# Paired exponentials over a ring of score chunks in a multi-expert attention stage

## The chip, the cores and the metric

The kernel runs on one core of a Trainium2 chip. The core has five engines that run side by side, each with its own instruction queue in program order: TensorE (PE, with its weight loads shown apart as PEld), VectorE (DVE), ScalarE (ACT), GpSimd (POOL) and SyncE (SP, which here issues DMAs). Semaphores tie them together: an instruction that needs another engine's result waits at the head of its queue, and everything behind it waits as well.

The metric is device time in microseconds (us) of one launch. Before the change it is 2863.09 us, the median of three runs (2863.0 to 2865.14).

## The reference, cut to what matters

A two-layer network on 3327 tokens with 256 features. Each layer is a graph step followed by a feed-forward block. The last block, `_L1_ffn_ref`, is the one that matters here. It is an attention with 4 heads of 64 features, and for each head 4 "experts", which have queries of their own but share keys and values:

```python
q = jnp.einsum('bnsd,neod->bneso', sx, wq)
k = jnp.einsum('bnsd,nod->bnso', sx, wk)
v = jnp.einsum('bnsd,nod->bnso', sx, wv)
causal = jnp.where(jnp.tril(jnp.ones((s, s), bool)), 0.0, -jnp.inf).astype(x.dtype)
scores = jnp.einsum('bnesd,bntd->bnest', q, k) * d ** 0.5 + causal
att = jax.nn.softmax(scores, axis=-1)
qkv = jnp.einsum('bnest,bntd->bnesd', att, v)
```

After it the experts are mixed by a gate, and a normalization, two small matrix products, a second normalization and a last gate follow. All of it is float32.

## The kernel before

The work is cut into 26 token tiles of 128 rows. The first stages (graph step, mixture of experts, second graph step) fill about the first 985 us. The change lies in the last stage, the method `heads`.

**Units and chunks.** A unit is one token tile `t` and one head `h`: 104 units in order of `t`, then `h`. Because attention is causal, a unit's keys are tiles 0 to `t`. They are cut into `t // 4 + 1` chunks of at most four tiles (512 columns), made about even by `span`. There are 392 chunks in one list, and a chunk is written `(u, g)`, with `g` its number in the unit.

**What happens to a chunk.** Five helpers work on it:

- `fill`: TensorE makes the scores of four experts in four PSUM banks (`pqk`), which all small products of the stage share.
- `drain`: VectorE copies the four score blocks out of PSUM into a tile `sc` of 4 x 512 columns and takes each row's maximum (`mx`). Where the chunk is the unit's last, it adds the causal mask, and the negated maximum over all chunks, `nmax` (in the profile `anmax`), is made.
- `weigh`: ScalarE takes the exponential in place, one instruction for each expert, and adds each row up into `den` (in the profile `aden`). Each such instruction is followed by a read of the accumulator. It needs `nmax`, and so the drains of all chunks of the unit.
- `turn`: VectorE transposes the chunk in 32 x 32 blocks, all four experts in one instruction.
- `attend`: TensorE multiplies the turned weights with the values `vr`, fetched by SP from DRAM, and adds up in one PSUM area `po`.

When a unit ends, `over` copies `po` to `ot` (ScalarE) and masks it (GpSimd), or does both on VectorE for `t` under 5; `back`, a round later, multiplies it with a matrix and ScalarE copies the result, `qkv`.

**Rounds.** The order of the work is written out by hand in one loop over the chunks, and a wrapper (`InOrder`) keeps each engine's instructions in the order in which the code makes them. One round, for chunk `k`, does: drain ahead; `attend` chunk `k`; `turn` the next chunk, or from tile 5 to about tile 23 the one after it (`extra`); fetch values; the first two exponentials of a chunk ahead (chunk `k + 2 + extra(k)`), if it is not the first of its unit; `back` and `over` where they are due; one step of the preparation of the next token tile (`run(preps)`) and one step of each unfinished tail (`run(tails)`); the remaining exponentials of the chunk ahead; ScalarE's small put-off operations (`quiet`); one `fill`. In a round that follows a unit's end, from tile 8 on, `run(preps)` and `run(tails)` are left out. A chunk with `g == 0` gets all four exponentials at the later place.

A tail is a generator that takes a finished token tile through gate, normalizations and small products, a step a round. Steps that matter for GpSimd's queue are the third (the gate's weights, products with `qkv` and sums into `fx`), the seventh and a later one (a normalization: `l1ns`, `l1rs`, `fx`, later `l2ns`, `l2rs`, `fo`), and `nonzero`, a comparison (`nz`, `nzf`).

**Buffers.** `sc` tiles come from a pool of nine buffers (`scp`); a buffer is used again when `attend` has read it. The queries of the first five token tiles (`qts`) are also kept in tiles of this pool. `den` has three buffers and is not cleared: each of its columns is written by one exponential.

Of the kernel before, what the change touches and what calls it, by code (L numbers as in the profile page):

```python
# [12 lines left out]
F32 = mybir.dt.float32  # L13
# [9 lines left out]
P = 128  # L23
# [5 lines left out]
BLK = 512  # L29
# [72 lines left out]
class Net:  # L102
# [753 lines left out]
    def heads(self, xs, vs, out):  # L856
        tc, a = self.tc, self.a
        nc = InOrder(tc)
        Q = 32
        with ExitStack() as ctx:  # L860
            one = ctx.enter_context(tc.tile_pool(name="at", bufs=1))
            self.work = ctx.enter_context(tc.tile_pool(name="atw", bufs=2))
            scp = ctx.enter_context(tc.tile_pool(name="ats", bufs=9))
            vrp = ctx.enter_context(tc.tile_pool(name="atv", bufs=3))
            tl = ctx.enter_context(tc.tile_pool(name="att", bufs=2))
            sm = ctx.enter_context(tc.tile_pool(name="atsm", bufs=4))
# [5 lines left out]
            )  # L872

            kt = one.tile([P, 4, NP], F32, name="kt")


            load = dict(act=0.0, dve=0.0)
# [30 lines left out]
            def prepare(t, res):  # L908
# [77 lines left out]
                yield  # L986
                if t < AHEAD:

                    qt = scp.tile([P, 4, BLK], F32, tag="sc", name="qts")[:, :, : 2 * P]
                    qt = qt.rearrange("p h (i q) -> p h i q", i=2)  # L990
                else:
                    qt = tl.tile([P, 4, 2, P], F32, tag="qt", name="qt")
# [42 lines left out]
            def span(t, g):  # L1035


                n = t // 4 + 1
                lo, hi = (t + 1) * g // n, (t + 1) * (g + 1) // n
                return lo, hi - lo  # L1040
# [15 lines left out]

            def drain(u, g):

                n = span(u["t"], g)[1] * P
                last = g == u["t"] // 4  # L1060
                if g == 0:
                    u["sc"] = {}
                    u["mx"] = sm.tile([P, 4, 8], F32, tag="mx", name="mx")
                sc = u["sc"][g] = scp.tile([P, 4, BLK], F32, tag="sc", name="sc")
                for e in range(4):
                    s, m = u["pq"][e][:, :n], u["mx"][:, e, g : g + 1]
                    if last:
                        nc.vector.tensor_tensor_reduce(
                            sc[:, e, :n], s, mask[:, BLK - n :], 1.0, NEG, ALU.add, ALU.max, m
                        )  # L1070
                    else:
                        nc.vector.tensor_scalar(
                            sc[:, e, :n], s, 1.0, None, ALU.mult, ALU.max, accum_out=m
                        )
                    load["dve"] += 0.12 + 0.00104 * n
                if last:
                    u["nmax"] = sm.tile([P, 4], F32, tag="nmax", name="anmax")
                    nc.vector.tensor_reduce(
                        u["nmax"], u["mx"][:, :, : g + 1], AX.X, ALU.max, negate=True
                    )  # L1080
                    load["dve"] += 0.2

            def weigh(u, g, experts):

                n = span(u["t"], g)[1] * P
                q = ready[u["t"]]
                if u["h"] == g == 0 and 0 in experts:
                    q["den"] = sm.tile([P, 16, 7], F32, tag="den", name="aden", bufs=3)
                for k in experts:
                    e = u["sc"][g][:, k, :n]  # L1090
                    nc.scalar.activation(
                        e, e, AF.Exp, bias=u["nmax"][:, k : k + 1],
                        accum_out=q["den"][:, 4 * u["h"] + k, g : g + 1],
                    )
                    load["act"] += 0.26 + 0.00088 * n

            def values(u, g):

                lo, n = (4 * i for i in span(u["t"], g))
                v = u["v", g] = vrp.tile([P, 16, 64], F32, tag="vr", name="vr")  # L1100
                for q in range(4):
                    nc.sync.dma_start(out=v[ds(Q * q, Q), :n, :], in_=vs[u["h"], :, lo : lo + n, :])

            def turn(u, g):


                n = span(u["t"], g)[1] * P
                w = u["sc"][g][:, :, :n]
                nc.vector.transpose(w, w)
                load["dve"] += 0.1 + 0.00417 * n  # L1110

# [6 lines left out]
            def attend(u, g):  # L1118


                t = u["t"]
                w, v = u["sc"][g], u["v", g]
                lo, n = (4 * i for i in span(t, g))
                for b2 in range(0, n, 2):
                    for k in range(2):
                        for q in range(4):
                            r, b = ds(Q * q, Q), b2 + k

                            after = 4 * t + q - lo
                            if b > after and t:  # L1130
                                continue
                            nc.tensor.matmul(
                                po[ds(64 * k, 64), q, :, :], v[r, b, :], w[r, :, ts(b, Q)],
                                start=(g == b2 == 0), stop=(b + 2 > after if t else b2 == 2),
                            )
# [307 lines left out]
                nc.sync.dma_start(out=out[ts(t, P), :], in_=fo)  # L1443

            units = [dict(t=t, h=h) for t in range(NT) for h in range(4)]
            chunks = [(u, g) for u in units for g in range(u["t"] // 4 + 1)]
            def begin(u):

                t = u["t"]
                if u["h"] == 0:  # L1450
                    if t == 0:
                        for _ in prepare(0, ready.setdefault(0, {})):
                            quiet()
                    while preps and "qt" not in ready[t]:
                        run(preps)
                        quiet()
                    begun = [t + 1] if AHEAD <= t + 1 < NT else []
                    if t + 2 < AHEAD:
                        begun = [t + 2] if t else [1, 2]
                    for i, n in enumerate(begun):  # L1460
                        preps.append(later(4 * i, prepare(n, ready.setdefault(n, {}))))
                u.update(ready[t])
# [3 lines left out]
            def fill_next():  # L1466
                nonlocal filled
                if filled < len(chunks):
                    u, g = chunks[filled]
                    if g == 0:  # L1470
                        begin(u)
                    fill(u, g)
                    filled += 1

            def drain_to(n):
                nonlocal drained
                while drained < min(n, len(chunks)):
                    if filled == drained:
                        fill_next()
                    drain(*chunks[drained])  # L1480
                    drained += 1

            def extra(k):

                t = chunks[min(k + 3, len(chunks) - 1)][0]["t"]
                return int(chunks[k][0]["t"] >= 5 and t // 4 + 1 <= 6)

            def wanted(k):

                c = min(k + 2 + extra(k), len(chunks) - 1)  # L1490
                return k + 3 + extra(k) + chunks[c][0]["t"] // 4
# [4 lines left out]
            drain_to(wanted(0))  # L1496
            for k in range(2):
                values(*chunks[k])
                weigh(*chunks[k], range(4))
            turn(*chunks[0])  # L1500
            fill_next()
            ended, flipped, weighed = None, 1, 2
            for k, (u, g) in enumerate(chunks):
                drain_to(wanted(k))
                attend(u, g)
                while flipped < min(k + 2 + extra(k), weighed, len(chunks)):
                    turn(*chunks[flipped])
                    flipped += 1
                if k + 2 < len(chunks):
                    values(*chunks[k + 2])  # L1510
                rest = []
                while weighed < min(k + 3 + extra(k), len(chunks)):
                    c = chunks[weighed]
                    if c[1]:
                        weigh(*c, range(2))
                    rest.append((*c, range(2 if c[1] else 0, 4)))
                    weighed += 1
                if ended:
                    back(ended)
                last = u if g == u["t"] // 4 else None  # L1520
                if last:
                    over(u)
                if not ended or u["t"] < 8:
                    run(preps)
                    run(tails)
                ended = last
                for c in rest:
                    weigh(*c)
                quiet()
                if filled == drained:  # L1530
                    fill_next()
# [557 lines left out]
```

## Time and profile before

The profiled execution took 2863.94 us by itself, with a span of 2862.2 us, and lies 0.85 us above the median of the three runs.

| engine | busy us | share of the span | in the 1650 us from 1150 to 2800 |
|---|---|---|---|
| TensorE | 2665.0 | 93% | 1607.63 |
| VectorE | 2368.9 | 83% | 1600.73 |
| ScalarE | 1790.0 | 63% | 1237.74 |
| GpSimd | 1075.3 | 38% | 599.39 |

How to read the profile. "Busy" counts an instruction from its start to its end. TensorE's matmuls are pipelined and their ends are modelled, so its busy share says little about how near it is to its limit. A group of instructions is shown as line, engine, operation, what is written and from what, shapes and count; then the busy time in us, the mean of one in ns, and the idle time of the engine just before, with what ended it. All instructions of this stage have the wrapper's line, L61, so they are told apart by the names of their tiles. A line of waits tells who waited for whom: us in total, how many times, the longest. A line of the timeline tells the start in us, the duration, the engine, the instruction, and in brackets the idle time before it with what ended it. The chain that ended last is followed back from the last instruction to what released it, step by step.

### The profile page before, as it was taken

What the parts mean: (1) busy time and instruction counts of PE and PEld (TensorE: products, weight loads), DVE (VectorE), ACT (ScalarE), POOL (GpSimd) and SP (SyncE); (2) the same over time, 40 slices, a digit from 0 to 9 for tenths busy, and PEclk for the clock granted to TensorE, in tenths of its full rate; (3) what the DMA queues carried; (4) which work ended last, traced back from release to release, by engine and by line L of the source; (5) the groups of instructions that cost most, each with busy time, mean ns of one, the idle gap of its engine ahead of it and who ended that gap; (6) DMA issues with size and microseconds to landing.
All of it is one profiled execution on the core that took longest, in us unless ns stands there. A gap on an engine that the chain in (4) does not pass through costs nothing.

```text
span 2862.2 us, 125012 instructions
## 1 busy us (share of the span) xinstructions
PE 2665.0 (93%) x53422; PEld 1979.1 (69%) x53422; DVE 2368.9 (83%) x5525; ACT 1790.0 (63%) x5130; POOL 1075.3 (38%) x1562
## 2 busy tenths in 40 slices
PE   7999988878989899999999999999999999999995
PEld 5888877756767666676666666666666666666664
DVE  5203643589999588899999999999999999999996
ACT  6510135555555367777777777777777777777774
POOL 5541644532132137755444333333233222223122
PEclk9999999999999799999999999999999999999998
DMA  9994568657775232333433443434343444434332
GB/s 381 388 337 138 180 217 266 209 183 247 275 273 180 73 94 84 109 108 116 116 111 113 119 121 114 116 118 121 114 127 116 120 120 119 123 116 122 117 107 78
DMA packets 258188, 449.69 MB, mean 157 GB/s; under 512 B 58816, under 2 KB 156608, under 8 KB 257504
## 3 DMA queue, kind: packets, MB, share of 16 engines
q1 hardware_dynamic: 245536, 417.50, 46.0%
q0 software_dynamic: 6576, 18.02, 1.7%
q8 instruction: 420, 6.88, 1.0%
q10 hardware_dynamic: 5520, 6.18, 0.6%
q14 instruction: 136, 1.11, 0.1%
HBM read 393.37 MB, written 25.88 MB: 146 GB/s over the span
## 4 chain that ended last, share of the span: by engine, by line
DVE 35%; PE 28%; ACT 3%; issue 2%; POOL 1%; DMA 0%; SPq 0%; POOLq 0%; DVEq 0%; ACTq 0%
DVE sc L61 32%; PE pqk L61 10%; PE po L61 10%; PE acc L61 2%; ACT sc L61 2%; PE ptO L61 2%; PE psxt L61 1%; PE pt L61 1%; PE pq L61 1%; PE ph L61 0%; ACT sq L61 0%; PE pk L61 0%; PE pv L61 0%; DVE anmax L61 0%; DVE gl L61 0%
## 5 line engine op out<-in xcount | busy, mean ns | idle before, releaser
L61 ACT ACTIVATE sc<-sc,anmax 128x512 f32<-128x512 f32 (+3 forms) x1568 | 1041.4, 669 | 102.9 <-DVE anmax L61 102.9
L61 PEld LDWEIGHTS po<-sc,vr 32*64 32x64 f32 x43728 | 662.5, 131 | 299.1 <-issue 147.6
L61 DVE STREAM_TRANSPOSE sc<-sc 128x2048 f32<-128x2048 f32 (+3 forms) x392 | 816.0, 2082 | 9.7 <-ACT sc L61 9.4
L61 PE MATMUL po<-sc,vr 32*64 32x128 f32 x43728 | 761.1, 276 | 31.6 <-DVE sc L61 21.5
L61 PE MATMUL pqk<-kt,qt 64*128 64x512 f32 (+1 forms) x2944 | 764.4, 585 | 19.0 <-DVE fgs L61 6.6
L61 DVE TENSOR_SCALAR_CACHE_REDUCE sc<-pqk 128x512 f32<-128x512 f32 (+2 forms) x1152 | 653.1, 621 | 26.0 <-PE pqk L61 23.8
L61 PEld LDWEIGHTS pqk<-kt,qt 64*128 64x128 f32 x2944 | 315.9, 185 | 239.5 <-issue 80.9
L61 PE MATMUL acc<-wh,p 128*128 128x259 f32 x1352 | 309.2, 386 | 35.6 <-DVE p L61 35.6
L61 PEld LDWEIGHTS acc<-wh,p 128*128 128x128 f32 x1352 | 253.2, 190 | 93.4 <-DVE p L61 53.3
L61 PE MATMUL acc<-y,pan 128*128 128x256 f32 x1352 | 298.4, 382 | 1.7 <-issue 1.7
L61 ACT ACTIVATION_READ_ACCUMULATOR sc<-sc,anmax 128x1 f32 x1568 | 299.5, 191 | 0.0
L61 PEld LDWEIGHTS acc<-y,pan 128*128 128x128 f32 x1352 | 257.2, 191 | 38.7 <-issue 3.2
L61 POOL TENSOR_TENSOR ot<-ot,sxd 128x512 f32<-128x512 f32 x83 | 105.9, 1276 | 436.2 <-ACT ot L61 431.1
L61 DVE CUSTOM_DVE_ANT_0 sc<-pqk,mask 128x512 f32<-128x512 f32 (+3 forms) x416 | 241.9, 636 | 25.4 <-PE pqk L61 24.6
L61 ACT ACTIVATE u<-u,d 128x512 f32<-128x512 f32 (+1 forms) x182 | 125.2, 688 | 159.2 <-DVE u L61 159.1
L61 DVE SCALAR_TENSOR_TENSOR u<-bc,d 128x512 f32<-128x512 f32 (+1 forms) x182 | 136.0, 748 | 0.1
L61 DVE SCALAR_TENSOR_TENSOR p<-pan,u 128x512 f32<-128x512 f32 (+1 forms) x182 | 126.1, 693 | 10.3 <-PE acc L61 6.1
L61 ACT COPY qkv<-ptO 128x272 f32<-128x272 f32 x104 | 39.7, 381 | 131.0 <-PE ptO L61 130.8
L61 PE MATMUL ptO<-igw,ot 128*128 128x68 f32 x832 | 115.7, 282 | 3.8 <-DVE sc L61 2.1
L61 PEld LDWEIGHTS ptO<-igw,ot 128*128 128x128 f32 x832 | 101.5, 192 | 22.5 <-issue 15.2
L61 ACT ACTIVATE junk<-ar 128x1664 bf16<-128x1664 f32 x52 | 82.8, 1592 | 54.1 <-DMA ar<-in_adj_dram 53.6
L61 DVE CUSTOM_DVE_ANT_0 sg<-sg,dst 128x1664 bf16<-128x1664 bf16 (+2 forms) x56 | 100.1, 1796 | 1.2 <-ACT dst L61 1.0
(356 smaller groups left out, 3082.0 us busy)
## 6 DMA issues: line engine op xcount, KB each, us to landing
vr<-vs SPq DMA_DIRECT2D x976, 128.0 KB
ar<-in_adj_dram SPq DMA_DIRECT2D x104, 832.0 KB
vr<-vs SPq DMA_DIRECT2D x544, 96.0 KB
pan<-in_adjt_dram SPq DMA_DIRECT2D x156, 256.0 KB
pan<-in_adjt_dram SPq DMA_DIRECT2D x26, 1024.0 KB
pan<-in_adjt_dram SPq DMA_DIRECT2D x20, 832.0 KB
w1e<-w SPq DMA_DIRECT2D x59, 256.0 KB
took<-places SPq DMA_DIRECT2D x59, 129.0 KB
```

Of the source, the lines that this page charges most:

```text
L61: made = make(*args, **kw)
```

## The change

The nine score buffers become one tile, `ring`, with the four experts as rows of 9 x 512 columns. Chunk number `c` has slot `c % 9`, and `c % 6` for the first 24 chunks, while the queries of the first five token tiles lie in the last three slots. Two neighbouring chunks of a unit, an even `g` and the one after it, form a pair where their slots are neighbours. The first of a pair is put at the right end of its slot, so that an expert's scores of both chunks lie side by side, and one exponential takes both, with one sum for both. The columns of `den` that no exponential writes any more have to be zero, so `den` is cleared by GpSimd for each token tile. Where a pair does not begin a unit, its first two exponentials are put into the round ahead, one early and one late, and the other two into its own round, again one early and one late. Chunks without a partner are treated as before. `turn` and `attend` go on chunk by chunk.

```diff
-            scp = ctx.enter_context(tc.tile_pool(name="ats", bufs=9))
...
+            RING = 9
+            ring = one.tile([P, 4, RING * BLK], F32, name="ring")
...
-                    qt = scp.tile([P, 4, BLK], F32, tag="sc", name="qts")[:, :, : 2 * P]
+                    qt = ring[:, :, ds(6 * BLK + 2 * P * t, 2 * P)]
...
             def drain(u, g):
 
+                c = u["c"] + g
                 n = span(u["t"], g)[1] * P
+                at = slot(c) * BLK + (BLK - n if paired(c) else 0)
                 last = g == u["t"] // 4
                 if g == 0:
-                    u["sc"] = {}
+                    u["sc"], u["at"] = {}, {}
                     u["mx"] = sm.tile([P, 4, 8], F32, tag="mx", name="mx")
-                sc = u["sc"][g] = scp.tile([P, 4, BLK], F32, tag="sc", name="sc")
+                sc = u["sc"][g] = ring[:, :, ds(at, n)]
+                u["at"][g] = at
...
-            def weigh(u, g, experts):
-
+            def slot(c):
+
+                return c % (RING if c >= 24 else 6)
+
+            def paired(c):
+
+                u, g = chunks[c]
+                return g % 2 == 0 and g < u["t"] // 4 and slot(c) + 1 == slot(c + 1)
+
+            def weigh(c, experts):
+
+                u, g = chunks[c]
                 n = span(u["t"], g)[1] * P
+                if paired(c):
+                    n += span(u["t"], g + 1)[1] * P
                 q = ready[u["t"]]
                 if u["h"] == g == 0 and 0 in experts:
                     q["den"] = sm.tile([P, 16, 7], F32, tag="den", name="aden", bufs=3)
+                    nc.gpsimd.memset(q["den"], 0.0)
                 for k in experts:
-                    e = u["sc"][g][:, k, :n]
+                    e = ring[:, k, ds(u["at"][g], n)]
                     nc.scalar.activation(
                         e, e, AF.Exp, bias=u["nmax"][:, k : k + 1],
                         accum_out=q["den"][:, 4 * u["h"] + k, g : g + 1],
...
-                w = u["sc"][g][:, :, :n]
+                w = u["sc"][g]
                 nc.vector.transpose(w, w)
...
                 rest = []
-                while weighed < min(k + 3 + extra(k), len(chunks)):
-                    c = chunks[weighed]
-                    if c[1]:
-                        weigh(*c, range(2))
-                    rest.append((*c, range(2 if c[1] else 0, 4)))
-                    weighed += 1
+                until = min(k + 3 + extra(k), len(chunks))
+                while weighed < until:
+                    left = range(begun, 4)
+                    if chunks[weighed][1]:
+                        half = len(left) // 2
+                        weigh(weighed, left[:half])
+                        left = left[half:]
+                    rest.append((weighed, left))
+                    weighed += 2 if paired(weighed) else 1
+                    begun = 0
+                if weighed < len(chunks) and chunks[weighed][1] and paired(weighed) and not begun:
+                    if not rest or rest[0][1][0] > 1:
+                        weigh(weighed, range(1))
+                        rest.append((weighed, range(1, 2)))
+                        begun = 2
```

Left out of the diff: the chunk list, which now notes each unit's first chunk number in `u["c"]`, and the two calls ahead of the loop, which follow the new arguments of `weigh`.

More of the change, by code (lines that the diff above doesn't have):

```diff
@@ L1445, in heads @@
             units = [dict(t=t, h=h) for t in range(NT) for h in range(4)]
-            chunks = [(u, g) for u in units for g in range(u["t"] // 4 + 1)]
+            chunks = []
+            for u in units:
+                u["c"] = len(chunks)
+                chunks += [(u, g) for g in range(u["t"] // 4 + 1)]
             def begin(u):
@@ L1498, in heads @@
                 values(*chunks[k])
-                weigh(*chunks[k], range(4))
+                weigh(k, range(4))
             turn(*chunks[0])
             fill_next()
-            ended, flipped, weighed = None, 1, 2
+            ended, flipped, weighed, begun = None, 1, 2, 0
             for k, (u, g) in enumerate(chunks):
```

## The prediction

> **What bounds the kernel now.** I read the busy table, the chain that ended last, the busy times of the heads stage, the waits of VectorE, the groups by shape, and the timeline around one exponential that starts late. The heads stage runs from about 985 us to the end.
>
> ```profile
> PE 2665.0 (93%) x53422; PEld 1979.1 (69%) x53422; DVE 2368.9 (83%) x5525; ACT 1790.0 (63%) x5130; POOL 1075.3 (38%) x1562
> DVE 35%; PE 28%; ACT 3%; issue 2%; POOL 1%; DMA 0%; SPq 0%; POOLq 0%; DVEq 0%; ACTq 0%
> ```
> ```profile
> 1150.00:2800.00 1650.00, 1607.63 (x45084) 1098.35 (x45082) 1600.73 (x3583) 1237.74 (x3902) 599.39 (x820) 1.00 0.40 117
> ```
> ```profile
> DVE sc L61 <- PE pqk L61: 47.6, 51, 4.5
> DVE sc L61 <- ACT sc L61: 9.4, 9, 3.6
> ```
> ```profile
> L61 ACT ACTIVATE sc<-sc,anmax 128x512 f32<-128x512 f32 x912 | 646.4, 713 | 18.6 <-DVE anmax L61 18.6
> L61 ACT ACTIVATION_READ_ACCUMULATOR sc<-sc,anmax 128x1 f32 x1328 | 253.0, 191 | 0.0
> L61 ACT ACTIVATE sc<-sc,anmax 128x384 f32<-128x384 f32 x416 | 250.7, 606 | 81.2 <-DVE anmax L61 81.2
> ```
>
> Over the whole program ACT is 3% of the chain. In the stretch from 1150 to 2800 us the third number after the width is VectorE: 1600.7 of 1650, or 97%. ScalarE is busy 1237.7 (75%). VectorE drains each score chunk out of PSUM (four instructions) and turns it (one transposition); it waits for the exponentials 9.4 us in the whole stage, nine times. So VectorE sets the pace, and an engine with a quarter of its time free is being relieved. What matters is *when* ScalarE answers.
>
> ```profile
> 2005.81 0.17 DVE L61 TENSOR_REDUCE anmax<-mx 128x4 f32<-128x20 f32 x1
> 2005.90 2.30 DVE L61 STREAM_TRANSPOSE sc<-sc 128x2048 f32<-128x2048 f32 x1
> 2006.02 0.61 ACT L61 ACTIVATE sc<-sc,anmax 128x384 f32<-128x384 f32 x1 [2.93 <-DVE anmax L61]
> ...
> 2008.34 0.18 ACT L61 ACTIVATION_READ_ACCUMULATOR sc<-sc,anmax 128x1 f32 x1
> ...
> 2010.01 1.77 DVE L61 STREAM_TRANSPOSE sc<-sc 128x1536 f32<-128x1536 f32 x1
> ```
>
> This is a unit's first chunk (g = 0). Its exponentials cannot start before `anmax`, which needs the unit's last chunk drained. ACT had waited 2.93 us for it. The four end at 2008.52, and VectorE reaches the chunk's transposition at 2010.01, after one older transposition and one drain. The slack is 1.49 us, fixed by VectorE's own order.
>
> **What the change takes away.** Counting the pairs by the new rule: 150 pairs, 600 exponentials and 600 accumulator reads fewer (1568 to 968 each). Starts of consecutive exponentials in the timeline lie 0.706 us apart for 512 columns and 0.599 for 384, reads included, because reads overlap the end; the difference of the two mean rows is 107 ns for 128 columns, 0.836 ns a column. So a pair of 512 costs 0.706 + 0.428 = 1.134 instead of 1.412, a saving of 0.278. No 1024-column exponential is in the trace; the line through two rows is the only price. 600 x 0.278 = 167 us of ScalarE, of which at most VectorE's 9.4 us of waits can return as time. Most of these lie in the last unit (1.95, 0.78, 0.47, 3.58, 1.60 us):
>
> ```profile
> 2814.71 2.31 DVE L61 STREAM_TRANSPOSE sc<-sc 128x2048 f32<-128x2048 f32 x1 [1.95 <-ACT sc L61]
> 2828.91 2.31 DVE L61 STREAM_TRANSPOSE sc<-sc 128x2048 f32<-128x2048 f32 x1 [3.58 <-ACT sc L61]
> ```
>
> There the exponentials of the last chunks stand behind small copies in ACT's queue. With half-pairs a round ahead the 3.58 us goes, but the first pair comes 1.2 us later, and the very last chunk is alone behind the `h` activation as now: I take 2 us gained, plus 1 us for the other waits. **-3 us.**
>
> **Pairs that begin a unit.** They cannot be started ahead; all four double exponentials follow `anmax`, and the first chunk's transposition now waits for the second chunk's columns too: 4 x 512 x 0.836 = 1.71 us later, or 1.28 with 384. Behind the waiting transposition stand VectorE's next drain and all else in its order; TensorE waits for both. There are 81 such pairs. From the timeline, end of the fourth read to start of the transposition, median slack by chunks a unit has:
>
> - 2 chunks (14 pairs): slack 1.30, added 1.50
> - 3 (16): 0.99, added 1.50
> - 4 (14): 1.41, added 1.71
> - 5 (14), 6 (16), 7 (7): 1.48, 1.46, 1.43, added 1.71
>
> Summed pair by pair, the excess is 46 us if exponentials begin where they begin now. With 2 to 4 chunks they now begin about 1 us after `anmax`, behind copies that wait for TensorE; if a lighter ACT begins all at `anmax`, the sum is 15 us. Waits for TensorE that already follow these transpositions absorb 8 or 3 of it. Ends: 38 and 12. Those copies wait for TensorE rather than for ACT's backlog, which speaks for the upper end; TensorE, running on during each stall, will come earlier, which speaks for the lower. I take **+20 us**.
>
> **Pairs that begin later in a unit** (g = 2, 4). Two exponentials move a round earlier and the other two hold the old deadline; the last wait shrinks from two singles (1.41) to one double (1.13). They pass ACT's copies `ot`, `qkv` and the small activations; no DMA, and nothing on SP, moves. Counting what is issued before the `ot` copy in a unit's last round: shorter in 41 rounds (17 us in all), longer in 11 (9 us). TensorE waits for `ot`, but VectorE is the bound: **0**, and at worst those 9 us.
>
> **The memset on POOL.** `den` is now cleared by GpSimd once per token tile (26 times), and the first exponential of the tile waits for it. The instruction is cheap (the 128x128 memset row took 0.20 us); its place is not. It is emitted after that round's `run(preps)` and `run(tails)`, so in POOL's order it stands behind their chains. For tile 2:
>
> ```profile
> 1029.92 0.61 ACT L61 ACTIVATE sc<-sc,anmax 128x384 f32<-128x384 f32 x1
> ...
> 1031.82 1.91 POOL L61 TENSOR_TENSOR qkv<-qkv,gss 128x1024 f32<-128x1024 f32 x1
> ...
> 1032.45 1.78 DVE L61 STREAM_TRANSPOSE sc<-sc 128x1536 f32<-128x1536 f32 x1
> ...
> 1035.98 0.73 POOL L61 TENSOR_TENSOR fx<-fx,sx 128x256 f32<-128x256 f32 x1
> ```
>
> Step 3 of tile 0's tail falls into that round and ends at 1036.7. The memset comes at 1036.9, four exponentials end at 1039.4, and the transposition that began at 1032.45 is 7.0 us late. By the same reading, tile 3 (two tail chains, to 1062.75) loses 7.8; tile 4 (to 1087.0) 8.9; tile 5 (norm chain to 1124.4) 4.4. Tiles 6 to 8 wait for the `ot` product (1.28 us): 1.5, 1.3, 1.9. Tile 15 loses 1.0 behind `nzf`, tiles 21 to 23 1.3 each behind `nz`. Elsewhere POOL is past the place before `anmax`. Sum 37.7. VectorE is idle 17% of 1000 to 1150 us, so a fifth of tiles 2 to 5 (28.1) is absorbed, and about 2 us is already counted with the first pairs. Ends: 0, if those chains finish before the round matters, and 38. I take **+30 us**, near the upper end, because the order is written in the code and the chains are in the trace.
>
> **The ring itself.** The same nine slots of 512 columns, six until chunk 24, when the early queries hold the rest. Drains, transpositions and matmuls keep count and size. Transpositions of 384 columns are strided already and cost 1.154 ns an element (1772 / 1536) against 1.125 contiguous (2305 / 2048): a wider stride gets **0**; were all 512-column ones strided at that rate, 244 x 0.06 = 15 us.
>
> **Sum.** -3 + 20 + 0 + 30 = +47 us on the profiled execution's own 2863.9 (span 2862.2), which lies 0.8 above the median of 2863.09: **2910 us**. Ends of the open terms: 12 + 0 - 3 = +9 and 38 + 38 - 3 + 9 = +82.
>
> [...]
>
> **Rivals.**
> (1) *Relief wins; faster.* If the transpositions' waits on ACT fall to none and copies such as `ot` and `qkv` come earlier for TensorE, the 9.4 us and a few of the 47.6 us of VectorE's waits on TensorE return: about -10, 2853. It decides if the g = 0 stalls and the memset together cost under 10 us. For it: ACT's 167 us. Against: VectorE's 97%. Chance 0.08.
> (2) *Nothing moves* (within 0.2%, 5.7 us, about what a measurement here can tell from no change): the costs meet the gain, or the engines' leads swallow both. 0.08.
> (3) *Only the late pairs cost*: the memset is passed in time, lower end of the stalls, +6 to +21, about 2876. 0.14.
> (4) *One tile orders more than nine did*: false waits between chunks sharing the ring, at 0.5 us for 350 chunks +175, 3040. Against: `kt`, written by parts while other parts are read, shows no such wait (ACT kt waits only for PE pk). 0.06.
> My forecast holds 0.64, with its own range 2884 to 2942.
>
> **Chances.** Slower by over 0.2%: 0.64 + 0.14 + 0.06 = 0.84; within 0.08; faster 0.08. The range runs 2869 to 2942: my forecast and (3), so 0.78; (1), (2) and (4) lie outside.
>
> **What would show it.** ACT's exponentials number 968 and ACT's busy time falls by about 165 us, to 1625. VectorE's work stays at 2369 us, while its waits for ACT's `sc` rise from 9.4 to 40 or more: near 1 us before first-chunk transpositions, and 4 to 9 us at tiles 2 to 5, with ACT waiting for POOL's `aden`. Wrong, if VectorE's waits on ACT stay under 15 us, if ACT never waits for `aden`, or if transpositions or drains change their mean.

## The result and the profile after

The changed kernel takes 2970.01 us (median of five runs, 2966.81 to 2971.82) against 2863.0 us before in the same comparison (2861.04 to 2865.14): ratio 1.0373, 95% interval 1.0358 to 1.0387, or 107 us slower. The forecast was 2910 with 2942 as its upper end: the direction was right, the size less than half. The profiled execution is the median one (2970.01 us by itself, span 2968.2).

The page of the changed kernel, its busy table and the first line of its chain:

```profile
PE 2717.6 (92%) x53422; PEld 2005.7 (68%) x53422; DVE 2376.2 (80%) x5525; ACT 1623.2 (55%) x3930; POOL 1078.5 (36%) x1588
...
PE 27%; DVE 26%; ACT 12%; issue 2%; POOL 2%; DMA 1%; SPq 0%; POOLq 0%; ACTq 0%; DVEq 0%
```

ScalarE was relieved of 166.8 us (1790.0 to 1623.2), and yet its share of the chain rose from 3% to 12%. It has less to do, and others wait for it more. TensorE has the same 53422 instructions and 52.6 us more busy time; VectorE has the same 5525 and 7.3 us more.

The groups by shape of the changed kernel (mean ns of one after the busy time) give the price of a double exponential:

```profile
L61 DVE STREAM_TRANSPOSE ring<-ring 128x2048 f32<-128x2048 f32 x244 | 562.3, 2305 | 27.9 <-ACT ring L61 27.4
...
L61 ACT ACTIVATE ring<-ring,anmax 128x896 f32<-128x896 f32 x300 | 309.3, 1034 | 120.0 <-DVE anmax L61 116.5 <-POOL aden L61 3.4
...
L61 ACT ACTIVATE ring<-ring,anmax 128x1024 f32<-128x1024 f32 x212 | 241.2, 1140 | 28.8 <-DVE anmax L61 27.3 <-POOL aden L61 1.5
...
L61 POOL MEMSET aden<- 128x112 f32 x26 | 5.0, 191 | 0.0
```

The line through the two shorter rows gives 713 + 512 x 0.836 = 1141 ns for 1024 columns, and 1140 came; starts of consecutive ones lie 1.133 us apart, where the prediction had 1.134. Transpositions of 2048 elements take 2305 ns as before, so the wider stride costs nothing here.

The waits of the changed kernel in the heads stage, from 980 us on (us in total, times, longest):

```profile
DVE ring L61 <- ACT ring L61: 85.3, 67, 9.9
...
DVE ring L61 <- PE pqk L61: 76.4, 77, 6.1
...
PEld pqk L61 <- ACT qkv L61: 34.3, 13, 7.8
...
ACT ring L61 <- POOL aden L61: 32.9, 9, 8.6
```

VectorE's waits for ScalarE rose from 9.4 to 85.3 us and its waits for TensorE's scores from 47.6 to 76.4. Together that is 105 us more, and the span grew by 106.0: nearly the whole loss is VectorE standing still (from 980 us on its idle time grew from 109.3 to 211.7 us). Sorting its idle time before turns by the chunk that is turned: before turns of first chunks in the first five token tiles 0.6 us became 27.2 (24.6 of it before a tile's very first turn, where the memset acts); before turns of first pairs in later tiles 0.7 became 49.1 (25.9 in heads 1 to 3, 23.2 in head 0, where the memset adds); in the last unit 8.4 became 9.6; before the later pairs it is 0.0 in both.

Tile 2 in the timeline of the changed kernel (start, duration, then idle time in brackets with what ended it):

```profile
1029.91 0.16 DVE L61 TENSOR_REDUCE anmax<-mx 128x4 f32<-128x4 f32 x1
...
1033.58 0.72 POOL L61 TENSOR_TENSOR fx<-fx,sx 128x256 f32<-128x256 f32 x1
1034.24 0.19 POOL L61 MEMSET aden<- 128x112 f32 x1
1034.47 0.61 ACT L61 ACTIVATE ring<-ring,anmax 128x384 f32<-128x384 f32 x1 [6.81 <-POOL aden L61]
...
1036.87 0.36 ACT L61 COPY qkv<-ptO 128x272 f32<-128x272 f32 x1
...
1037.29 1.91 PE L61 MATMUL pqk<-kt,ring 64*128 64x384 f32 x4 [5.17 <-ACT qkv L61]
```

A 0.19 us clear stands behind GpSimd's tail chain; ScalarE waits 6.81 us for it, and the copy `qkv`, queued behind the exponentials, keeps TensorE from its next scores for 5.17 us.

### The profile page after: what moved, and what is told of

The parts are those of the page before. It is cut to its first block, busy times and chain, and to the rows that moved or that the text cites. A ratio compares the mean times of both kernels' runs of the same rounds, so it can differ in the third digit from the quotient of the medians.

```text
span 2968.2 us, 123820 instructions
## 1 busy us (share of the span) xinstructions
PE 2717.6 (92%) x53422; PEld 2005.7 (68%) x53422; DVE 2376.2 (80%) x5525; ACT 1623.2 (55%) x3930; POOL 1078.5 (36%) x1588
## 4 chain that ended last, share of the span: by engine, by line
PE 27%; DVE 26%; ACT 12%; issue 2%; POOL 2%; DMA 1%; SPq 0%; POOLq 0%; ACTq 0%; DVEq 0%
DVE ring L61 24%; ACT ring L61 10%; PE po L61 10%; PE pqk L61 10%; PE ptO L61 2%; PE acc L61 2%; ACT sq L61 1%; PE pq L61 1%; PE psxt L61 1%; PE ph L61 1%; PE pt L61 1%; POOL qkv L61 1%; DMA vr<-vs 0%; POOL fx L61 0%; SPq L61 0%
## 5 line engine op out<-in xcount | busy, mean ns | idle before, releaser
L61 ACT ACTIVATE ring<-ring,anmax 128x896 f32<-128x896 f32 (+7 forms) x968 | 873.7, 906 | 188.0 <-DVE anmax L61 155.0
L61 PEld LDWEIGHTS po<-ring,vr 32*64 32x64 f32 x43728 | 677.8, 133 | 311.7 <-issue 133.6
L61 DVE STREAM_TRANSPOSE ring<-ring 128x2048 f32<-128x2048 f32 (+3 forms) x392 | 816.0, 2083 | 85.9 <-ACT ring L61 85.3
L61 PE MATMUL pqk<-kt,qt 64*128 64x512 f32 (+1 forms) x2944 | 787.8, 595 | 48.9 <-ACT qkv L61 7.7
L61 PE MATMUL po<-ring,vr 32*64 32x128 f32 x43728 | 778.3, 280 | 36.8 <-DVE ring L61 17.2
L61 DVE TENSOR_SCALAR_CACHE_REDUCE ring<-pqk 128x512 f32<-128x512 f32 (+2 forms) x1152 | 654.3, 622 | 53.7 <-PE pqk L61 52.4
L61 DVE CUSTOM_DVE_ANT_0 ring<-pqk,mask 128x512 f32<-128x512 f32 (+3 forms) x416 | 241.9, 636 | 25.0 <-PE pqk L61 24.8
L61 ACT ACTIVATION_READ_ACCUMULATOR ring<-ring,anmax 128x1 f32 x968 | 184.9, 191 | 0.0
L61 PEld LDWEIGHTS ptO<-igw,ot 128*128 128x128 f32 x832 | 102.9, 195 | 24.6 <-issue 12.5
L61 ACT COPY ot<-po 128x512 f32<-128x512 f32 x83 | 48.0, 578 | 115.1 <-PE po L61 113.1
```

Of the source, the lines that this page charges most:

```text
L61: made = make(*args, **kw)
```

## The experiments

Every kernel was compared with the kernel before on the same chip. A difference in us is ratio minus one, times 2863.

| kernel | ratio to before, 95% | us |
|---|---|---|
| as changed | 1.0373 [1.0358, 1.0387] | +107 |
| memset early | 1.0186 [1.0172, 1.0201] | +53 |
| no first pairs | 1.0306 [1.0286, 1.0326] | +88 |
| both | 1.0156 [1.0142, 1.0171] | +45 |
| memset alone | 1.0142 [1.0122, 1.0162] | +41 |
| ring alone | 0.9997 [0.9988, 1.0007] | -1 |
| first pairs alone | 1.0109 [1.0092, 1.0126] | +31 |
| both, pairs in their own round | 1.0020 [1.0008, 1.0032] | +6 |
| both, copies ahead of the early exponentials | 1.0325 [1.0304, 1.0345] | +93 |
| before, one exponential ahead of `ot` | 0.9976 [0.9965, 0.9986] | -7 |
| before, three ahead of `ot` | 1.0066 [1.0053, 1.0080] | +19 |
| before, LIGHT = 6 | 1.0033 [1.0020, 1.0045] | +9 |
| own round, LIGHT = 6 | 1.0041 [1.0028, 1.0055] | +12 |

**The memset and the first pairs, each undone.** First the clear moves into `begin`, rounds ahead of its use:

```diff
 def weigh(c, experts):
-    if u["h"] == g == 0 and 0 in experts:
-        q["den"] = sm.tile(...)
-        nc.gpsimd.memset(q["den"], 0.0)
 def begin(u):
+    if u["h"] == 0:
+        den = sm.tile(...)
+        nc.gpsimd.memset(den, 0.0)
+        ready[t]["den"] = den
```

> The clearing of den is put where a token tile's queries are first used, rounds ahead of its first exponential; all pairs stay. Theory W (waits add up: the memset's place and the first pairs each cost what VectorE waits for them): the wait of ACT for aden (32.9 us) goes, with it 27 us of VectorE's waits in tiles 1 to 4 and some 15 us at first pairs of later tiles, so about 2925 us. Theory C (the waits let TensorE idle, its clock drops, and the fills come late): the same saving plus the share of half-clock time that goes with those waits, 143 us to 100 or less, so about 2910 us. Rival R (the one ring tile orders work that nine tiles left free): the larger part stays, 2940 us or more.

Measured: +53, between theory W (2925 us is +62) and theory C (2910 is +47). The place of one 0.19 us instruction is worth 54 of the 107 us. Next, first pairs are left single:

```diff
-    return g % 2 == 0 and g < u["t"] // 4 and slot(c) + 1 == slot(c + 1)
+    return g % 2 == 0 and 0 < g < u["t"] // 4 and slot(c) + 1 == slot(c + 1)
```

> Chunks with g = 0 are never the first of a pair; pairs at g = 2 and 4 stay, the memset stays in its place. W: VectorE's waits for ACT outside the tiles' first units go (26 us), those of the first units shrink to what the memset costs alone; about 2905 us. C: half-clock time falls to 80 us or less and VectorE's waits for fills return from 76 to about 50 us; about 2895 us. R: 2940 us or more.

Measured: +88, so undoing first pairs here gives back 19 us. W (+42) and C (+32) both missed; only R's 2940 us or more fits, and the ring alone, below, rules R out. Then both edits together:

> Both edits: den cleared early and no pairs at g = 0; the ring, the pairs at g = 2 and 4 and their half a round ahead stay. W and C: VectorE waits for ACT under 10 us, half-clock time as before (38 us), time 2855 to 2866 us. R: above 2880 us.

Measured: +45, a miss again: W and C, for which memset and first pairs were all, had 2855 to 2866 us and so left nothing. A third cost was missing. VectorE's timeline showed where it lies: tiles 0 to 10 take as long as before to 0.5 us. The loss begins at the end of tile 11, when the units of tile 12, the first with a pair past their first chunk, come into ScalarE's queue, and goes on to the end. And the memset alone, on the kernel before:

```diff
                     q["den"] = sm.tile([P, 16, 7], F32, tag="den", name="aden", bufs=3)
+                    nc.gpsimd.memset(q["den"], 0.0)
```

> The kernel before with one line more, the memset of den on GpSimd at the place where the changed kernel has it; nine separate tiles, no pairs. W: 30 to 38 us over before, 2893 to 2901 us, with VectorE waiting 7 to 9 us once in each of the tiles 2 to 4. C: the same or up to 10 more, with half-clock time in tiles 1 to 5. R: no more than 5 us over before.

Measured: +41 (35 to 46 by the interval), over W's 30 to 38 and inside C's 10 more. In its profile the durations of tiles 1 to 4 grow by 6.9, 7.2, 9.3 and 4.5 us.

**The third cost.** In the kernel with both edits VectorE waits for exponentials hardly more than before (11.6 us against 9.4). It waits for TensorE (waits from 980 us on):

```profile
DVE ring L61 <- PE pqk L61: 91.9, 94, 4.2
...
DVE ring L61 <- ACT ring L61: 11.6, 8, 4.8
```

Its timeline shows one such place:

```profile
2670.01 1.11 PE L61 MATMUL ptO<-igw,ot 128*128 128x68 f32 x8
...
2672.48 1.03 ACT L61 ACTIVATE ring<-ring,anmax 128x896 f32<-128x896 f32 x1
...
2673.50 1.03 ACT L61 ACTIVATE ring<-ring,anmax 128x896 f32<-128x896 f32 x1
2674.53 0.36 ACT L61 COPY qkv<-ptO 128x272 f32<-128x272 f32 x1
...
2674.95 0.95 PE L61 MATMUL pqk<-kt,qt 64*128 64x384 f32 x2 [2.34 <-ACT qkv L61]
...
2675.94 0.56 DVE L61 TENSOR_SCALAR_CACHE_REDUCE ring<-pqk 128x384 f32<-128x384 f32 x1 [2.38 <-PE pqk L61]
```

The product `ptO` was done at 2671.12. ScalarE fetches it at 2674.53, behind what was left of four short squares (to 2672.48) and two double exponentials, of chunks that VectorE turns only from 2676.42 and 2687.04 us on. The bank it occupies is one that the next scores need: TensorE loses 2.34 us, VectorE 2.38. So the theory became: ScalarE's small copies out of PSUM are what TensorE waits for, and exponentials issued half a pair ahead stand in front of them. Four kernels test it. The ring alone (`paired` returns false, no memset):

> The ring with its slots and addresses, but no pairs, no memset and nothing ahead: every chunk has its four exponentials as before. Theory Q (what is left with both waits removed, 44 us, is ScalarE's queue: half of a pair put a round ahead stands in front of the copies of po and of the small products, for which TensorE waits): the ring costs nothing, 2863 to 2871 us. R (the ring orders more): 2885 us or more, with the loss in tiles 12 to 25, where the run with both edits has it.

Measured: -1, no difference. One tile in place of nine buffers cost nothing measurable here (ratio 0.9997, 0.9988 to 1.0007). Then the kernel with both edits, and no half of a pair ahead:

```diff
-                if weighed < len(chunks) and chunks[weighed][1] and paired(weighed) and not begun:
-                    if not rest or rest[0][1][0] > 1:
-                        weigh(weighed, range(1))
-                        rest.append((weighed, range(1, 2)))
-                        begun = 2
```

> As the run with both edits (den cleared early, no pairs at g = 0), but a pair's four exponentials all stay in its own round, two early and two late; nothing is put a round ahead. Between anmax and the copy of po into ot ScalarE then has about 7.3 us of exponentials in units of 4 and 5 chunks, where it has 6.6 before and 8.3 with half ahead. Q: TensorE's wait for ot falls from 20 us to under 10 and the time to 2880 to 2895 us. R: unchanged, about 2910 us.

Measured: +6 against +45, less than the 2880 to 2895 us that Q had. Half a pair ahead costs 39 us; doubling the later exponentials costs almost nothing by itself. Its waits from 980 us on:

```profile
DVE ring L61 <- PE pqk L61: 56.7, 61, 4.5
...
PEld po L61 <- ACT ot L61: 6.7, 8, 1.3
```

VectorE's waits for TensorE fell from 91.9 to 56.7 us, and TensorE's for `ot` from 20.1 to 6.7, as Q had it. And the kernel with both edits, with `back` and `over` moved up, ahead of the early exponentials:

```diff
+                if ended:
+                    back(ended)
+                last = u if g == u["t"] // 4 else None
+                if last:
+                    over(u)
                 rest = []
                 until = min(k + 3 + extra(k), len(chunks))
```

> As the run with both edits, with half of a pair ahead, but in each round back and over (the copies qkv and ot) are issued before the early exponentials. Q: TensorE's wait for ot falls below 10 us, but ScalarE now waits for attend before the early exponentials, so part of the gain goes: 2880 to 2905 us. R: unchanged, about 2910 us.

A miss: +93, 48 us worse than without the move, although TensorE's wait for `ot` did fall, from 20.1 to 5.2 us. ScalarE keeps the order of the code, so where a copy is queued before its product exists, what stands behind it waits too. The timeline of this kernel in tile 10, which has no pairs in it:

```profile
1377.26 1.98 PE L61 MATMUL ptO<-igw,ot 128*128 128x68 f32 x8
...
1379.27 0.39 ACT L61 COPY qkv<-ptO 128x272 f32<-128x272 f32 x1 [5.47 <-PE ptO L61]
1379.56 0.62 ACT L61 ACTIVATE ring<-ring,anmax 128x384 f32<-128x384 f32 x1
```

ScalarE idles 5.47 us with four exponentials behind the copy. The clock may have a part in it: the granted clock was 0.50 in the windows from 1376 to 1382 us, and the eight matmuls of `ptO` took 1.98 us there, where they took 1.11 in the place above, in the kernel with both edits. The last of the four is the first pairs alone, with the memset early:

```diff
-    return g % 2 == 0 and g < u["t"] // 4 and slot(c) + 1 == slot(c + 1)
+    return g == 0 < u["t"] // 4 and slot(c) + 1 == slot(c + 1)
```

> Den cleared early; pairs only at g = 0, which nothing puts a round ahead. The prediction's term alone: 81 late pairs at 12 to 38 us, so 2879 to 2905 us, all of it as VectorE's wait for ACT. Q adds that ScalarE has less in front of ot (5.6 us instead of 6.6), so TensorE's waits stay as before and the time is in the lower half, 2879 to 2892 us. R: 2905 us or more.

Measured: +31, inside the prediction's 12 to 38 and just over the lower half that Q had named (+16 to +29). Its waits from 980 us on:

```profile
DVE ring L61 <- ACT ring L61: 50.1, 63, 3.1
DVE ring L61 <- PE pqk L61: 48.6, 48, 6.2
```

VectorE's waits for ScalarE rise by 40.7 us over before (9.4), and its waits for TensorE stay where they were (47.6). That is the reverse of the third cost: two different mechanisms.

**The order alone.** The next two take the kernel before, with its nine tiles and single exponentials, and move one exponential of a later chunk across the copies.

```diff
-                    if c[1]:
-                        weigh(*c, range(2))
-                    rest.append((*c, range(2 if c[1] else 0, 4)))
+                    if c[1]:
+                        weigh(*c, range(1))
+                    rest.append((*c, range(1 if c[1] else 0, 4)))
```

> The kernel before, its nine tiles and single exponentials kept; of a later chunk's four exponentials one instead of two is issued ahead of the copy `ot`, the other three behind it. Queue theory (what counts is how much exponential work ACT holds between a unit's `anmax` and its `ot` copy): 0.7 us less ahead of the copy, so TensorE gets `ot` sooner, but where the copy itself waits for TensorE's `po`, three exponentials instead of two now stand behind that wait; the kernel with none ahead lost 51 us against two ahead. Between these ends: 2850 to 2890, taken 2868. Rival (VectorE's own work sets the pace, and ACT's order does not matter as long as VectorE does not wait for ACT): within 0.2% of before.

> The kernel before, with three of a later chunk's four exponentials issued ahead of the `ot` copy instead of two. No instruction is added, removed or paired. Queue theory: the ACT work between `anmax` and `ot` rises from 6.5 to about 7.2 us; the half-a-pair-ahead block raised it from 7.3 to 8.3 and more and cost 38 us, so about 38 us for each us over it: 20 to 30 us slower, taken 2890, and the loss stands in VectorE's drains waiting for TensorE's scores, not in VectorE waiting for ACT. Rival (the loss came from the doubled instructions themselves, or from VectorE waiting for exponentials): within 0.2% of before, since the last exponential of every chunk ends no later.

Measured: one ahead -7, three ahead +19 (just under the 20 to 30 expected). The rival, no more than 0.2% from before, is excluded by three ahead, and by one ahead (0.14% to 0.35% faster) it is not. No instruction was added, removed or resized: the order of ScalarE's queue alone is worth 26 us between the two. The profiled execution of one ahead took 2868.55 us, more than its median of 2862.18 and more than that of before, so its trace does not show where the gain lies. The waits of the kernel with three ahead:

```profile
DVE sc L61 <- PE pqk L61: 71.5, 81, 4.2
...
DVE sc L61 <- ACT sc L61: 9.1, 9, 2.7
```

Against before (47.6 and 9.4), the loss is again VectorE waiting for TensorE, with not one microsecond more for the exponentials.

The lateness of these copies can be counted: from the end of a product's last matmul (ends are modelled) to the start of ScalarE's copy of it, less 0.1 us, summed over eleven kinds of results that ScalarE fetches from PSUM in the heads stage (a twelfth, the queries `qt`, is not in the sums). For kernels without first pairs and with the clear out of the way, each from its one profiled execution:

| kernel | copies' lateness, us | time against before, us |
|---|---|---|
| one ahead of `ot` | 89 | -7 |
| before | 115 | 0 |
| own round | 127 | +6 |
| three ahead of `ot` | 163 | +19 |
| both edits, half a pair ahead | 208 | +45 |
| both edits, copies moved up | 228 | +93 |

The two orders agree, which is no proof of the cause. The ring alone fits (113 us and -1). The two kernels of the next test have 146 us (+9) and 165 (+12), the last out of order beside three ahead. `ot` alone does not rank the kernels: own round and three ahead have it equally late (29.5 and 29.6 us) and lie 13 us apart, while `qkv` (13.6 and 21.9) and `kt` (4.7 and 12.5) differ. The count also fits the miss: moving `ot` up did make `ot` early (59.7 to 15.3 us of lateness), and it made the other copies behind it late (`kt` 10.7 to 30.1, `fo` 7.8 to 19.9). That this is the whole of the last row is argued, not shown.

**Can the freed ScalarE time be spent?** One constant decides up to which token tile the small statistics and softmaxes are done on VectorE. It was lowered in the kernel before, as a control, and in the best kernel with pairs:

```diff
-            LIGHT = 16
+            LIGHT = 6
```

> The kernel before with one constant changed: the token tiles that do their small statistics and softmax work on VectorE end at tile 5 instead of tile 15, so tiles 6 to 15 do it on ACT and GpSimd. Control for the next one. If ACT's queue is what holds TensorE, ACT (75% busy in 1150 to 2800 us) takes this badly: 0 to 25 us slower. If VectorE's 97% is what holds, it is faster by up to VectorE's work moved, some 1 to 2 us a tile, 10 to 20 us.

> The kernel with pairs only past a unit's first chunk, taken in their own round, and the early memset (2873.96 us), with the same constant changed as in the control: it spends the ScalarE time that the pairs freed on work taken from VectorE. If freed ScalarE time is worth anything, it is here: 2850 to 2870, and better than the control changes the kernel before. If only the order of ACT's queue counts, it moves as the control does or worse: 2874 to 2895.

Measured: +9 for the control, +12 with pairs, which is +6 on top of the +6 that this kernel had. Work moved from the 97% engine, most of it to the 75% engine, makes both slower, by about as much: the time that the pairs freed does not pay for it. In the control VectorE's busy time fell by 15.2 us (2368.9 to 2353.7) and its waits for TensorE rose from 47.6 to 69.8: less work for the engine called the bound did not make the kernel faster.

## Why the prediction was wrong, point by point

**ScalarE's relief, -3.** The 167 us of busy time was right (166.8). The gain was not there: waits in the last unit went from 8.4 to 9.6 us.

**Pairs that begin a unit, +20 of 12 to 38.** Right in kind, low in size: 31 alone, with 38.1 us of waits before these turns. The upper end, "exponentials begin where they begin now", was the better reading. In the whole change they cost less (about 9 on top of the later pairs, ratios 1.0186 against 1.0156; 19 with the memset in place). With chunk 1 drawn into the first pair, its exponentials no longer stand in front of `ot`: that copy's lateness is 59.7 us without first pairs and 26.1 with them (memset early in both).

**Pairs that begin later, "0, and at worst those 9 us".** This step failed, and taken alone it is the largest error: 45 measured, 39 of it from the half taken ahead. Added to first pairs it is 22 (53 against 31). It failed twice. The count of what stands before `ot` took a unit's last round alone; but ScalarE's backlog builds up from `anmax`, when four exponentials of the next unit's first chunk are released at once. Counted in the traces from `anmax` to the start of `ot` (each exponential at 0.28 us plus 0.836 ns a column, the line of the prediction's start-to-start times; medians of units of four, five and six chunks), about 6.6 us of exponentials stand ahead of `ot` before, 7.3 to 7.4 with pairs in their own round, and 8.3 to 9.4 with half ahead. And "VectorE is the bound" was used as a reason why TensorE's wait costs nothing. VectorE at 97% has no work in stock: it drains what TensorE has just made, TensorE needs the bank that ScalarE empties, and a late copy passes through both within a microsecond, as the 2.34 and 2.38 us show in one place. The control with `LIGHT` agrees.

**The memset, +30 of 0 to 38.** Place and sizes were right, the sum was not. For tiles 2 to 5 the working gave 7.0, 7.8, 8.9 and 4.4; the memset alone cost 6.9, 7.2, 9.3 and 4.5. (The waits come before the first turns of tiles 2 to 5 and so lengthen tiles 1 to 4.) The step that failed is "a fifth of tiles 2 to 5 is absorbed": nothing is. VectorE's 17% of idle time between 1000 and 1150 us did not take any of it up. Alone the memset costs 41, and its interval of 35 to 46 takes in the upper end of 38; in the whole change 43 (88 against 45) to 54. The `qkv` copy behind the late exponentials holds TensorE too: its waits for that copy rose from 6.6 to 31.1 us with the memset alone. How much of the cost beyond 38 comes that way is not shown.

**The ring, 0.** Right. The 0.5 us a chunk that rival (4) took for false waits was the author's assumption; no run shows it, and the ring alone measured -1 us.

**What would show it.** 968 exponentials and 1623 us came; VectorE's waits for ScalarE went past 40, to 85; ScalarE waits for `aden` 32.9 us in nine places. But the signs named nothing for TensorE, and the rise in VectorE's waits for it (28.8 us) is one half of the 60 us that the forecast lacked. The other half is in the waits for ScalarE, which rose by 75.9 us where the sum had 47.

**The rivals.** That relief wins, that nothing moves, and false waits on the ring all fell. Rival (3) left only the first pairs, at the lower end of their stalls, with the memset passed in time; the clear was not passed in time, and the later pairs cost too.

The reading of VectorE as the engine that sets the pace was right in this: nearly all of the loss is idle time of VectorE (from 980 us on 109.3 us before, 211.7 after). What the sum lacked are the gaps on that engine and what ends them. Before the change 47.6 us of its waits ended on TensorE and 9.4 on ScalarE; the prediction priced the smaller.

How the three costs share the 107 is not quite a sum: alone they are 41 + 31 + 45 = 117. Added one after the other along the table they are 31 (first pairs), 22 (later pairs on top) and 54 (the memset's place); in another order the shares differ.

The range does not quite follow from the prediction's own working either: +82 on 2863 is 2945, not 2942. That changes nothing here.

## What to carry to other kernels

Relief of an engine off the bound is judged by the order of its queue: for every short instruction that another engine waits for, count the work that stands ahead of it, from the moment at which that work is released. Prefetching into such a queue is paid for by what then stands behind it, here 39 us for half a pair and 19 us for one exponential; putting the short ones first failed too (+93 us), since their inputs were not ready and the queue then waited, 5.47 us in the place shown. A tiny instruction on a side engine cost what its queue held in front of it, here up to 9 us for 0.19 us of work.

The kernel before with one exponential ahead of `ot` instead of two is the fastest measured, 0.24% (0.14% to 0.35%) under before; of the change itself no part made a faster kernel.

## What the runs showed of the hardware

TensorE's granted clock was 0.50 for more of the heads stage after the change than before. One such place, in the windows of the changed kernel from 2338 us on (width, busy time and count of each engine in the order PE, PEld, DVE, ACT, POOL, then the granted clock, DMA share and GB/s):

```profile
2338.00:2342.00 4.00, 1.95 (x13) 1.10 (x12) 1.64 (x3) 4.00 (x10) 0.00 (x0) 1.00 0.52 153
2342.00:2344.00 2.00, 2.00 (x4) 0.61 (x4) 1.97 (x8) 2.00 (x5) 0.00 (x0) 0.58 0.44 104
2344.00:2346.00 2.00, 2.00 (x50) 1.34 (x57) 1.66 (x5) 0.96 (x2) 0.00 (x0) 0.50 0.21 49
2346.00:2348.00 2.00, 2.00 (x81) 1.97 (x68) 1.69 (x1) 0.00 (x0) 0.00 (x0) 0.50 0.03 8
2348.00:2350.00 2.00, 2.00 (x18) 1.27 (x13) 0.00 (x0) 1.16 (x4) 0.92 (x1) 0.72 0.32 88
```

And two lines of its timeline there:

```profile
2341.82 2.91 PE L61 MATMUL pqk<-kt,qt 64*128 64x512 f32 x4 [2.05 <-ACT v L61]
...
2350.29 0.69 DVE L61 TENSOR_SCALAR_CACHE_REDUCE ring<-pqk 128x512 f32<-128x512 f32 x1 [2.60 <-PE pqk L61]
```

TensorE had paused for 2.05 us, behind the copy `v` in ScalarE's queue. In the four windows from 2342 to 2350 us the granted clock was 0.58, 0.50, 0.50 and 0.72, and VectorE's drain of the next chunk waited 2.60 us. That the pause brought the lower clock is the author's reading; the trace shows only what came after what. Between 1010 us and 60 us before the end the stretches at a granted clock of 0.50 sum to 112.6 us in 20 places after the change and 13.7 us in 4 before. TensorE's 52.6 us more of busy time for the same matmuls is about half of the difference of 98.9, but busy time does not measure the clock alone: with the copies moved up it is 59.9 more than before at a mean granted clock of 0.966, where the changed kernel has 0.959 (before: 0.976).

How much of the 107 us is the clock and how much the waits was not separated. If all time at 0.50 were matmuls that a granted clock of 1.00 had done in half of it, the clock itself would cost half of the difference of 98.9: an estimate of at most 49 us of the 107. What follows from that lost time is not in this figure. With both edits (+45) and with three ahead of `ot` (+19) the mean granted clock of the profiled execution was 0.974, close to the 0.976 of before; what it cost there was not worked out. With `LIGHT = 6` it was 0.981 in the kernel before and 0.979 with pairs, no lower than before, and both are slower all the same: there the clock is not the cause.
